# Residual rows and stores of a graph layer: from one DMA queue to halves on two

## The chip, the cores and the metric

The kernel runs on one core of a Trainium2 chip. A core has five engines with a queue of instructions each: TensorE (PE in the profile, its weight loads PEld), VectorE (DVE), ScalarE (ACT), GpSimd (POOL) and SyncE (SP), and 16 DMA engines that all queues share. A DMA is issued by an instruction in the queue of SyncE, ScalarE or GpSimd; an engine's instructions start in their written order, so one that waits holds up all that are queued behind it. The metric is the device time of one execution in microseconds (us).

## The reference

Eight batches of 4096 nodes with 256 features go through one layer of a graph network with a residual connection and a layer norm. With the setup's sizes it is:

```python
HW = jnp.einsum('bnf,fo->bno', H, W)              # H = x: 8 x 4096 x 256, W: 256 x 256
A_norm = jax.nn.relu((A + A.T) * 0.5)             # A = adj: 4096 x 4096, mostly zeros
D = jnp.sum(A_norm, axis=1)
d_inv_sqrt = jnp.where(D > 0, jnp.where(D > 0, D, 1.0) ** (-0.5), 0.0)
DAD = d_inv_sqrt[:, None] * A_norm * d_inv_sqrt[None, :]
L_norm = jnp.eye(N) - DAD
gnn = jax.nn.relu(jnp.einsum('nm,bmo->bno', L_norm, HW))
x = layernorm(x + gnn, axis=-1)                   # no scale or shift, eps 1e-5
```

All numbers are float32.

## The kernel before

**First stage.** The adjacency matrix is symmetrised tile by tile (512 x 512) and written to a scratch array `a_dram` in memory, by DMAs in ScalarE's queue (line 513); the features are multiplied by the weights, scaled and written to `g_dram` (8 KB a node: 8 batches of 256 features), also from ScalarE's queue (lines 622 and 633). The product for the first block of 128 output nodes, `lead`, is summed alongside. Which nodes have any neighbour in which block is noted, and lists of the nodes that matter are made from that.

**Second stage.** The other 31 blocks of 128 output nodes are worked on in 16 units, in the order of `SEQ`: 1 to 7, then 0, then 8 to 15. Unit u holds the blocks 2u+1 and 2u+2 (unit 15 only block 31). For each unit a list of nodes is gathered from memory in tiles of 128: GpSimd issues, per tile, an indirect DMA for pieces of `a_dram` (`ga`, line 944) and one for rows of `g_dram` (`g`, line 952, 1 MB). The tiles lie in a ring of 12 buffers (`RING`), so gathers run ahead of the products.

TensorE's work of a unit is cut into *steps*, written out by `steps_of`. A step is either one full tile (128 rows and columns of the array, four matmuls of 512 columns) or a *tiled* step, in which eight small products, 64 rows by 32 columns, share the array, in four rounds `m`. After each round of a tiled step ScalarE gets an empty instruction, a *tick* (line 1198), that waits for the round's first products; the products of a later round wait for the tick before last. So ticks pass through ScalarE's queue, and TensorE can be at most two rounds ahead of it in tiled steps. Full-tile steps have no ticks.

When a block's last product is done, `finish` is called: ScalarE evicts the four banks to the one buffer `y` with ReLU and the row's scale (`evict`, line 760). One step later follows `rest` on VectorE: it adds `y` to the residual rows (line 770), takes the moments (779, 781), an inverse root by three Newton steps, and normalises in place (line 803, eight instructions, one for each batch). The rows of `x` that are added lie in buffers `xr` of 1 MB, 128 nodes by 8 batches by 256 features; the pool `adj` has four of these. The last block (31) has its own `finish_last`, which evicts (line 1010), adds (1018, 1020, 1026), normalises on ScalarE (1042) and stores in four parts (1049). Its residual rows are loaded by GpSimd's queue into a free ring buffer.

**Order of the work around the change.** Each instruction of the second stage is put, with `queue(...)`, directly behind the one before on its engine. `after(n, fn)` notes a function for later; `run_later(2)` is called once at the end of each step and counts all notes down by two, so `after(2, ...)` means one step on and `after(6, ...)` the third `run_later` from the note. At a new unit the notes are made ahead of that step's own count, so `after(6, ...)` comes at the end of the unit's third step, counted 2 from 0.

Residual rows of blocks 0, 3 and 4 are asked for between the stages, and of block 5 in unit 1's first step. From then on a store brings a load with it: `LATE` = 4, two steps after a block's `rest`, SyncE's queue gets the store of that block (line 813) and behind it the load (line 754) of the block three places further on in `line`, the order in which blocks are finished. A load waits until the buffer's last store has landed. All 31 loads and 31 stores, 1 MB each in pieces of 1 KB, are in SyncE's queue, and ScalarE issues no DMA in this stage.

DMAs of SyncE and ScalarE share eight semaphores in turn: an issue first waits until the DMA that used its semaphore before, eight issues earlier over both queues, has landed.

Of the kernel before, what the change touches and what calls it, by code (L numbers as in the profile page):

```python
# [9 lines left out]
F32 = mybir.dt.float32  # L10
# [13 lines left out]
SEQ = [1, 2, 3, 4, 5, 6, 7, 0, *range(8, 16)]  # L24
# [43 lines left out]
def kernel(  # L68
# [25 lines left out]
    nc = tc.nc  # L94
    B, N, F = x.shape
    FO = w.shape[1]
    P = 128
# [11 lines left out]
    HOLD = 10  # L109
    RING = 12  # L110
    REACH = 5
    LATE = 4
    EPS = 1e-5
    NK = len(KINDS)
    L = 64
# [3 lines left out]
    def blocks(u):  # L119

        return min(2, NB - 1 - 2 * u)
# [104 lines left out]
    for s in range(NE):  # L226
        h = slice((s % QU) * E, (s % QU + 1) * E)
# [240 lines left out]
    blocks_pool = ctx.enter_context(tc.tile_pool(name="adj", bufs=4))  # L468
# [283 lines left out]
    def residual(i, engine):  # L752
        xr = blocks_pool.tile([P, B, F], F32, tag="adj", name=f"xr_{i}")
        engine.dma_start(xr, x[:, i * P : (i + 1) * P, :].rearrange("b p f -> p b f"))
        return xr

    def evict(i, py, ypool):
        y = ypool.tile([P, B, FO], F32, tag="y", name=f"y_{i}", bufs=1)
        for c in range(G // S):
            nc.scalar.activation(  # L760
                y.rearrange("p b o -> p (b o)")[:, c * S : (c + 1) * S],
                py[c],
                AF.Relu,
                scale=minus_r[:, i : i + 1],
            )
        return y

    def moments(i, y, z, stat):

        nc.vector.tensor_add(z, z, y)  # L770
        return statistics(i, z, stat)
# [40 lines left out]
    def store(i, z):  # L812
        nc.sync.dma_start(out[:, i * P : (i + 1) * P, :].rearrange("b p f -> p b f"), z)
# [72 lines left out]
    with (  # L886
# [33 lines left out]
        def queue(engine):  # L920

            traced = reversed(nc.cur_bb.bb.instructions)
            return tc.issue_after(next(i for i in traced if i.engine == engines[engine]))
# [55 lines left out]
        def after(n, fn, *args):  # L979
            later.append((n, fn, args))  # L980

        def run_later(by):
            ready = [l for l in later if l[0] <= by]
            later[:] = [(n - by, fn, args) for n, fn, args in later if n > by]
            for _, fn, args in ready:
                fn(*args)


        line = [0, *(2 * u + 1 + b for u in SEQ for b in range(blocks(u)))]
        u = SEQ[0]  # L990
        xr = {i: residual(i, nc.sync) for i in (0, *range(2 * u + 1, 2 * u + 1 + blocks(u)))}
        for h in range(max(HUBS)):
# [58 lines left out]
        def finish(i):  # L1051

            if i == NB - 1:
                while later:
                    run_later(1)
                finish_last(i)
                return
            with queue("act"):
                y = evict(i, py.pop(i), ypool)

            def rest():
                z = xr.pop(i)
                with queue("dve"):
                    mv, var = moments(i, y, z, stat)
                with queue("dve"):
                    rstd = inverse_root(i, var, stat)

                def end():
                    in_turn(normalise, i, z, mv, rstd)
                    after(LATE, store_late)  # L1070

                def store_late():
                    with queue("sp"):
                        store(i, z)
                    n = line.index(i) + 3
                    if 3 < n < len(line) - 1:
                        residuals([line[n]])

                end()

            after(2, rest)

        def residuals(rows):
            for i in rows:
                with queue("sp"):
                    xr[i] = residual(i, nc.sync)


        ahead = {u: {k: SEQ[n + k] for k in (2, 3, 4) if n + k < NU} for n, u in enumerate(SEQ)}
# [51 lines left out]
        def in_turn(fn, *args):  # L1141

            with queue("dve"):
                fn(*args)

        finish(0)
        ticks = []

# [52 lines left out]
        for q, (u, step) in enumerate(steps):  # L1201
            new = q == 0 or steps[q - 1][0] != u
            if new:
                after(6, prepare, u)
                if q == 0:
                    after(2, residuals, [line[3]])
                left, begun = {}, set()
                for v, st in steps[q:]:
                    if v == u:
                        for _, _, b, j in st:  # L1210
                            for e in range(QU) if j is None else [j]:
                                left[b, e] = left.get((b, e), 0) + 1
                for b in range(blocks(u)):
                    py[2 * u + 1 + b] = []
            touched = sorted({b for _, _, b, _ in step})
            for b in touched:
                if not py[2 * u + 1 + b]:
                    py[2 * u + 1 + b] = [
                        psum.tile([P, S], F32, tag=f"b{b}", name=f"py_{u}_{b}_{c}") for c in range(NC)
                    ]  # L1220
            if step[0][1] is None:
                (op,) = step
                b = op[2]
                hs = {(b, e) for e in range(QU)}
                assert not hs & begun or hs <= begun
                for h in hs:
                    left[h] -= 1
                for c in range(NC):
                    product(
                        u, op, c, slice(0, P), slice(0, P), not hs & begun, not any(left[h] for h in hs)  # L1230
                    )
                begun |= hs
            else:
                for op in step:
                    assert op[2:] in begun
                    left[op[2:]] -= 1
                last = [op for op in step if not left[op[2:]]]
                tiled(u, step, last)
            for op in step:
                t = op[0]  # L1240
                uses_left[u, t] -= 1
                if t < 0:
                    load_hub_rows(SEQ[SEQ.index(u) + 1 :], -1 - t, op[2])
            gather_ahead()
            run_later(2)
            for b in touched:
                if not any(left[b, e] for e in range(QU)):
                    if b == 0:
                        after(2, lists, u)
                    finish(2 * u + 1 + b)  # L1250
        while later:
            run_later(1)


    anyf = ipool.tile([P, 1], F32, tag="anyf", name="anyf")
# [4 lines left out]
    with tc.If(short > 0):  # L1260
        with (
# [4 lines left out]
            for i in range(NB):  # L1266
# [17 lines left out]
                z = residual(i, nc.scalar)  # L1284
                mv, var = moments(i, y, z, stat)
# [30 lines left out]
```

## Time and profile before

| | |
|---|---|
| median of 6 runs | 1511.1 us (1505.04 to 1515.72) |
| the profiled execution | 1512.02 us, span 1509.8 us, mean granted TensorE clock 0.968 |
| second stage, from TensorE's first `py` product | 594.9 us to the end |
| TensorE busy | 1378.6 us, 91% of the span |
| VectorE, ScalarE, GpSimd busy | 69%, 24%, 51% |
| DMA | 543.04 MB, mean 360 GB/s |
| queue of GpSimd (q0), SyncE (q1), ScalarE (q10) | 283.87, 156.25, 100.96 MB |
| evictions of a block, line 760 | 688 ns each, four to a block |
| addition of residual rows, line 770 | 2286 ns each |

The page's busy shares are means over two stages with different limits. In lists of groups a row has the line, engine and operation, what is written and read, the count, the busy time and the mean of one, and then the idle time before them with what ended most of it. In a timeline or chain the first number is the start in us after the span's start, the second the duration; square brackets hold the idle time before and what ended it. The starts of the units, from TensorE's records, are (us): unit 1 594.9, 2 678.3, 3 743.2, 4 804.2, 5 861.6, 6 915.4, 7 973.2, 0 1025.3, 8 1128.3, 9 1179.1, 10 1227.8, 11 1274.4, 12 1324.8, 13 1375.5, 14 1415.0, 15 1453.4.

### The profile page before, as it was taken

How to read it: one execution, taken by the hardware profiler on the slowest of the kernel's cores; microseconds unless marked ns; L12 is line 12 of the kernel's file. 1: busy time of each engine (PE TensorE's matmuls, PEld its weight loads, DVE VectorE, ACT ScalarE, POOL GpSimd, SP SyncE). 2: the span in 40 equal slices, each digit the busy share in tenths (PEclk: the TensorE clock that was granted, in tenths of full speed). 3: DMA queues.
4: the chain of work that ended last, by engine and by line, in shares of the span. 5: the costliest groups of instructions: out<-in, count | busy, mean ns of one | idle time of the engine just before them, and what ended most of it. 6: DMA issues, size and time to landing. Idle time of an engine off the chain costs nothing.

```text
span 1509.8 us, 29675 instructions
## 1 busy us (share of the span) xinstructions
PE 1378.6 (91%) x11008; PEld 746.2 (49%) x11008; DVE 1039.1 (69%) x3173; ACT 360.2 (24%) x462; POOL 769.8 (51%) x1564
## 2 busy tenths in 40 slices
PE   6999998989999979999999999999999998998962
PEld 5877877767777753343433433333333333333320
DVE  5676578979956462319486797798319898989426
ACT  3555544444445441000101101100001011011102
POOL 3444010011313325765765777767656677777741
PEclk9999999999999989999999999999999999999986
DMA  9999999999989999999999999999979999999993
GB/s 360 372 359 400 396 377 349 369 340 350 357 318 349 335 394 382 395 393 317 374 377 337 385 384 369 391 369 384 396 259 329 351 373 401 379 359 391 391 344 133
DMA packets 217158, 543.04 MB, mean 360 GB/s; under 512 B 19369, under 2 KB 109193, under 8 KB 182425
## 3 DMA queue, kind: packets, MB, share of 16 engines
q0 software_dynamic: 55664, 283.87, 49.2%
q1 hardware_dynamic: 122592, 156.25, 30.6%
q10 hardware_dynamic: 38752, 100.96, 17.1%
q8 instruction: 89, 1.46, 0.4%
q14 instruction: 61, 0.50, 0.1%
HBM read 438.03 MB, written 136.34 MB: 380 GB/s over the span
## 4 chain that ended last, share of the span: by engine, by line
PE 45%; DMA 26%; DVE 19%; issue 5%; POOL 2%; ACT 2%; ACTq 0%; SPq 0%; POOLq 0%; DVEq 0%
PE py L1163 28%; PE pg L607 8%; DMA g<-g_dram,gi 7%; DMA xr<-in_x_dram 4%; DMA a_dram<-sym 4%; DVE sym L500 4%; DMA out_dram<-xr 3%; DMA ga<-a_dram,ai 3%; PE lead L565 3%; PE tr L496 3%; DVE sums L507 2%; PE xtr L596 2%; DMA xin<-in_x_dram 2%; DVE stats L779 2%; DVE xr L770 1%
## 5 line engine op out<-in xcount | busy, mean ns | idle before, releaser
L1163 PE MATMUL py<-g,ga 64*32 64x512 f32 (+1 forms) x7136 | 614.2, 609 | 33.8 <-DMA g<-g_dram,gi 16.2
L1163 PEld LDWEIGHTS py<-g,ga 64*32 64x32 f32 (+1 forms) x7136 | 223.6, 113 | 407.5 <-issue 318.4
L952 POOL DMA_INDIRECT g<-g_dram,gi x268 | 298.6, 1114 | 115.6 <-issue 61.6
L944 POOL DMA_INDIRECT ga<-a_dram,ai x268 | 290.6, 1084 | 127.6 <-PE py L1163 61.9
L760 ACT ACTIVATE y<-py,minus_r 128x512 f32<-128x512 f32 x120 | 72.7, 688 | 807.8 <-PE py L1163 524.8
L607 PE MATMUL pg<-w_sb,xt 128*128 128x256 f32 x1024 | 229.4, 382 | 5.8 <-ACT xt L597 4.0
L1163 PE MATMUL py<-g_hub,gh 128*128 128x512 f32 x480 | 220.7, 601 | 5.2 <-DVE pos_k L240 5.2
L500 DVE TENSOR_TENSOR sym<-tr,adj 128x512 f32<-128x512 f32 x256 | 161.5, 680 | 82.0 <-PE tr L496 73.2
L607 PEld LDWEIGHTS pg<-w_sb,xt 128*128 128x128 f32 x1024 | 193.8, 192 | 33.6 <-ACT xt L597 4.4
L508 POOL TENSOR_SCALAR uses<-sums 128x64 uint8<-128x64 f32 x64 | 27.7, 432 | 312.0 <-DVE sums L507 263.6
L507 DVE TENSOR_REDUCE sums<-sym 128x64 f32<-128x2048 f32 x64 | 145.3, 2277 | 51.7 <-ACT sym L504 51.7
L496 PE MATMUL tr<-ident,adj 128*128 128x128 f32 x1024 | 139.7, 286 | 29.1 <-DVE sym L500 17.4
L1163 PEld LDWEIGHTS py<-g_hub,gh 128*128 128x128 f32 x480 | 87.6, 190 | 133.4 <-issue 120.7
L504 ACT ACTIVATE sym<-sym 128x2048 f32<-128x2048 f32 x64 | 122.8, 1918 | 127.7 <-DVE sym L500 127.7
L496 PEld LDWEIGHTS tr<-ident,adj 128*128 128x128 f32 x1024 | 119.7, 147 | 56.0 <-DVE sym L500 35.0
L443 DVE TENSOR_SCALAR low<-lists 128x17 f32<-128x17 f32 (+8 forms) x14 | 2.5, 175 | 197.3 <-PE lists L431 197.3
L770 DVE TENSOR_TENSOR xr<-xr,y 128x2048 f32<-128x2048 f32 x31 | 70.9, 2286 | 70.3 <-DMA xr<-in_x_dram 37.0
L596 PE MATMUL xtr<-ident,xin 128*128 128x128 f32 x512 | 72.4, 287 | 14.9 <-DVE sym L500 14.2
L565 PE MATMUL lead<-gt,strip 128*128 128x512 f32 x176 | 83.0, 594 | 3.3 <-ACT gt L617 3.3
L803 DVE TENSOR_SCALAR xr<-xr,mv,root 128x256 f32<-128x256 f32 x248 | 85.1, 413 | 1.1
L779 DVE BATCH_NORM_STATS2 stats<-xr 128x6 f32<-128x256 f32 x248 | 84.0, 412 | 1.1
L617 ACT ACTIVATE gt<-pg,r 128x512 f32<-128x512 f32 x88 | 60.1, 690 | 77.8 <-PE pg L607 68.1
(157 smaller groups left out, 1060.0 us busy)
## 6 DMA issues: line engine op xcount, KB each, us to landing
adj<-in_adj_dram SPq DMA_DIRECT2D x64, 1024.0 KB
a_dram<-sym ACTq DMA_DIRECT2D x64, 1024.0 KB
xr<-in_x_dram SPq DMA_DIRECT2D x31, 1024.0 KB
out_dram<-xr SPq DMA_DIRECT2D x31, 1024.0 KB
xin<-in_x_dram SPq DMA_DIRECT2D x44, 512.0 KB
g_dram<-gt ACTq DMA_DIRECT2D x22, 1024.0 KB
xin<-in_x_dram POOLq DMA_DIRECT2D x20, 512.0 KB
g_dram<-held ACTq DMA_DIRECT2D x10, 1024.0 KB
```

The lines of the kernel that those rows point to most:

```text
L496: ins = nc.tensor.transpose(pt[:, c * P : (c + 1) * P], tji[:, c, a * P : (a + 1) * P], ident)
L500: nc.vector.tensor_add(sym[:, a, :], pt, tij[:, a, :])
L504: nc.scalar.activation(sym, sym, AF.Relu, scale=0.5)
L507: nc.vector.tensor_reduce(sums, sym.rearrange("p a (c q) -> p a c q", q=E), AX.X, ALU.add)
L565: nc.tensor.matmul(lead[c], lhsT=strip, rhs=g[:, c * S : (c + 1) * S], start=not done, stop=len(done) == NB - 1, skip_group_check=True,)
L596: nc.tensor.transpose(pt[:, k, c, :], xin[b // H][:, b % H + k, c * P : (c + 1) * P], ident)
L607: ins = nc.tensor.matmul(pg[:, k * FO : (k + 1) * FO], lhsT=xt[:, b + k, c, :], rhs=w_sb[:, c, :], start=(c == 0), stop=(c == FC - 1),)
L770: nc.vector.tensor_add(z, z, y)
L779: nc.vector.bn_stats(stats[:, b, :], z[:, b, :])
L944: nc.gpsimd.indirect_dma_start(out=at if both else at[:, : E if one else P], out_offset=None, in_=a_pairs if both else a_groups if one els ...
L952: nc.gpsimd.indirect_dma_start(out=gt, out_offset=None, in_=g_dram, in_offset=bass.IndirectOffsetOnAxis(ap=gi[:, t : t + 1], axis=0), boun ...
L1163: return nc.tensor.matmul(py[2 * u + 1 + b][c][cols, :], lhsT=at[ps, off + cols.start : off + cols.stop], rhs=gt[ps, c * S : (c + 1) * S], ...
```

## The change

Every store of a block and every load of residual rows, but for the three loads between the stages and block 31, is cut into batches 0 to 3 and 4 to 7. One half is issued by SyncE, the other by ScalarE. They are issued in `exchange`: it takes the oldest block that is normalised and not stored (`finished`), stores it, batches 0 to 3 from SyncE, 4 to 7 from ScalarE, and then loads the rows of one block that it is told of, batches 0 to 3 from ScalarE, 4 to 7 from SyncE.

The times of issue change with it. In a unit of two blocks one exchange comes at the end of the third step and one at the end of the sixth, the first with the rows of the unit's own first block, the second with those of its second. Unit 1 has one exchange, at the end of its fourth step, with a store and no load; unit 15 has two without loads, at the ends of its first and second steps. Loads no longer hang on a store three blocks earlier, and block 5's early load in unit 1 is gone. What is left is stored at the end.

```diff
--- before.py
+++ after.py
@@ -109,7 +109,6 @@
     HOLD = 10
     RING = 12
     REACH = 5
-    LATE = 4
     EPS = 1e-5
     NK = len(KINDS)
     L = 64
@@ -986,7 +985,6 @@
                 fn(*args)
 
 
-        line = [0, *(2 * u + 1 + b for u in SEQ for b in range(blocks(u)))]
         u = SEQ[0]
         xr = {i: residual(i, nc.sync) for i in (0, *range(2 * u + 1, 2 * u + 1 + blocks(u)))}
         for h in range(max(HUBS)):
@@ -1053,6 +1051,8 @@
             if i == NB - 1:
                 while later:
                     run_later(1)
+                while finished:
+                    exchange([])
                 finish_last(i)
                 return
             with queue("act"):
@@ -1065,25 +1065,30 @@
                 with queue("dve"):
                     rstd = inverse_root(i, var, stat)
 
-                def end():
-                    in_turn(normalise, i, z, mv, rstd)
-                    after(LATE, store_late)
-
-                def store_late():
-                    with queue("sp"):
-                        store(i, z)
-                    n = line.index(i) + 3
-                    if 3 < n < len(line) - 1:
-                        residuals([line[n]])
-
-                end()
+                in_turn(normalise, i, z, mv, rstd)
+                finished.append((i, z))
 
             after(2, rest)
 
-        def residuals(rows):
+        def exchange(rows):
+
+            if finished:
+                i, z = finished.pop(0)
+                for h, (name, engine) in enumerate((("sp", nc.sync), ("act", nc.scalar))):
+                    bs = slice(h * B // 2, (h + 1) * B // 2)
+                    with queue(name):
+                        engine.dma_start(
+                            out[bs, i * P : (i + 1) * P, :].rearrange("b p f -> p b f"), z[:, bs]
+                        )
             for i in rows:
-                with queue("sp"):
-                    xr[i] = residual(i, nc.sync)
+                t = blocks_pool.tile([P, B, F], F32, tag="adj", name=f"xr_{i}")
+                for h, (name, engine) in enumerate((("act", nc.scalar), ("sp", nc.sync))):
+                    bs = slice(h * B // 2, (h + 1) * B // 2)
+                    with queue(name):
+                        engine.dma_start(
+                            t[:, bs], x[bs, i * P : (i + 1) * P, :].rearrange("b p f -> p b f")
+                        )
+                xr[i] = t
 
 
         ahead = {u: {k: SEQ[n + k] for k in (2, 3, 4) if n + k < NU} for n, u in enumerate(SEQ)}
@@ -1143,6 +1148,7 @@
             with queue("dve"):
                 fn(*args)
 
+        finished = []
         finish(0)
         ticks = []
 
@@ -1202,8 +1208,15 @@
             new = q == 0 or steps[q - 1][0] != u
             if new:
                 after(6, prepare, u)
+                rows = [2 * u + 1 + b for b in range(2)] if q > 0 and blocks(u) == 2 else []
                 if q == 0:
-                    after(2, residuals, [line[3]])
+                    after(8, exchange, [])
+                elif rows:
+                    after(6, exchange, rows[:1])
+                    after(12, exchange, rows[1:])
+                else:
+                    after(2, exchange, [])
+                    after(4, exchange, [])
                 left, begun = {}, set()
                 for v, st in steps[q:]:
                     if v == u:
@@ -1250,6 +1263,8 @@
                     finish(2 * u + 1 + b)
         while later:
             run_later(1)
+        while finished:
+            exchange([])
 
 
     anyf = ipool.tile([P, 1], F32, tag="anyf", name="anyf")
```

## The prediction

> **What bounds the kernel now.** I read the page first (busy shares, chain), then the chain in order of time, the table of waits, the timeline of the last 70 us and SyncE's own timeline; then I counted the matmul records of line 1163 off against the written order of steps, which gives the time of each step.
>
> ```profile
> span 1509.8 us, 29675 instructions
> PE 1378.6 (91%) x11008; PEld 746.2 (49%) x11008; DVE 1039.1 (69%) x3173; ACT 360.2 (24%) x462; POOL 769.8 (51%) x1564
> DMA  9999999999989999999999999999979999999993
> PE 45%; DMA 26%; DVE 19%; issue 5%; POOL 2%; ACT 2%; ACTq 0%; SPq 0%; POOLq 0%; DVEq 0%
> ```
>
> The second stage runs from 594.9 to the end. TensorE is its main bound: a step takes 3.5 to 3.6 us and the units 2 to 5 last little more than their steps. TensorE's pauses over 0.8 us between matmuls sum to about 56 us: 17.5 on gathers (3 us a unit in units 6, 7, 9, 10, 11), 16 on VectorE, and 15.3 in one piece. That piece is in unit 15. The table of waits (us in total, times, longest) and the chain show it:
>
> ```profile
> PE py L1163 <- ACTq L1198: 15.2, 1, 15.2
> ACT y L760 <- DVE xr L770: 167.7, 15, 32.7
> DVE xr L770 <- DMA xr<-in_x_dram: 37.0, 2, 24.3
> ```
>
> ```profile
> 538.19 23.46 DMA xr<-in_x_dram
> ...
> 1382.26 47.06 DMA out_dram<-xr
> 1429.34 42.09 DMA xr<-in_x_dram
> 1471.56 2.30 DVE xr L770
> ...
> 1482.47 2.21 DVE xr L770
> ```
>
> The residual rows arrive late: block 28's let VectorE wait 24.3 us (to 1447.6), block 29's 12.8 us (to 1471.6). There is one y buffer, so ScalarE can't evict block 30 until VectorE has read block 29's y; behind that eviction on ScalarE stand the ticks for which TensorE waits. The timeline of the end:
>
> ```profile
> 1447.64 2.29 DVE L770 TENSOR_TENSOR xr<-xr,y 128x2048 f32<-128x2048 f32 x1 [24.25 <-DMA xr<-in_x_dram]
> 1473.94 2.42 ACT L760 ACTIVATE y<-py,minus_r 128x512 f32<-128x512 f32 x4 [21.49 <-DVE xr L770]
> 1474.12 10.08 PE L1163 MATMUL py<-g,ga 64*32 64x512 f32 x128 [15.21 <-ACTq L1198]
> 1484.79 2.42 ACT L1010 ACTIVATE y<-py,minus_r 128x512 f32<-128x512 f32 x4 [8.42 <-DVE xr L770]
> 1493.20 0.68 DVE L1020 TENSOR_TENSOR g<-g,y 128x512 f32<-128x512 f32 x1
> ```
>
> The loads are late because SyncE's one queue is behind. Its timeline shows issues that should take 0.4 us held for 14 to 16:
>
> ```profile
> 1408.47 17.14 SPq L813 DMA_DIRECT2D out_dram<-xr  x1
> 1429.34 14.34 SPq L754 DMA_DIRECT2D xr<-in_x_dram  x1
> 1444.59 16.29 SPq L813 DMA_DIRECT2D out_dram<-xr  x1
> ```
>
> The packets say why. In 6 us between 1370 and 1388 GpSimd's gathers move some 285 packets (mostly 8 KB, 0.335 us each) and SyncE's queue 340 (1 KB, 0.049 us): about one turn each, so 1 MB of rows takes some 17 us. When the gathers stop at 1468 it takes 4.
>
> **The last units, with the change.** Every engine's program order is written out, so I can place the new instructions. Each exchange puts half a store and half a load on each queue. In the windows of the first stage where SyncE's and ScalarE's queues both work (545 to 550: 661 and 649 packets) they too get about equal turns. With two turns to the gathers' one, a round of 0.385 us for 1 KB becomes 0.435 for 2 KB: 1 MB in some 9.6 us where it took 17.
>
> Unit 14 starts at 1415.0. Its first exchange stands behind step 2 (+10.8 us), its second behind step 5 (+21.3). Blocks 27 and 29 move in the first: 2 MB, about 19 us and 2 to land: block 29's rows are there at 1448. VectorE wants them when block 29 is evicted, 31.6 + 2.6 us into the unit: 1449. Block 30's rows follow in the second exchange, about 1456 if a round is cheaper than I think, 1467 if the gathers last. VectorE is free for them 11.2 us after 1449, at 1460.4. So block 30's addition starts between 1460.4 and 1467; I take 1464, between the two because the gathers end near it. Before, the end hung on 1482.4.
>
> But the change also puts both stores into ScalarE's queue inside unit 15: block 29's after step 0, block 30's after step 1. They wait for VectorE's normalising, and the ticks of the next step are queued behind; TensorE gets two of a step's four rounds ahead and then stops. So from block 30's addition: 10.9 us to its normalising's end (1482.4 to 1493.3 here), 0.6 for the issue, 1.9 for the rest of step 2, 3.5 for step 3, 1.3 for two evictions, and the 16.6 us that now lie between line 1020's start at 1493.2 and the end: 34.8, and 1 for GpSimd's addition: 35.8. The ends are 1496.2, 1499.8 (for 1464) and 1502.8, against 1509.8: **-10 us, -13.6 to -7.**
>
> **The start of the stage.** The fourth early load goes (block 5's, issued at 546.3 and landed by 566). The chain runs through the third, 538.19 for 23.46 us: a DMA waits for the one that last used its semaphore, eight DMAs back over both queues, and ScalarE's store of a_dram issued at 561.7 waits so for the load of block 4. One DMA fewer shifts this by one: that store would wait for block 3's load, landed near 548, and ScalarE would be free at 554.6. But the next store then gets block 4's semaphore, and in ScalarE's queue its wait stands ahead of the second of four gt multiplications (562.74), so most of the stop stays: **-1.3 us**; bounds 0 and -7.5, the whole of the idle time there.
>
> **New waits on ScalarE in the other units.** An exchange costs ScalarE two issues, 0.4 to 0.5 us each by SyncE's unhindered ones, beside an engine that is 24% busy. What counts is the wait: the half store needs the normalising to be done. That ends 11 to 12 us into the next unit for block one (15 in units 4, 11, 12) and 22 to 23 for block two (26 there); the steps before the exchanges end at 10.8 and 21.4 (13 and 23.3). So ScalarE stands 1 to 3 us, and behind it are ticks alone. Full-tile steps need none, and a tiled step runs 1.7 us before it does. What is left over is 0.6 + 0.8 us in unit 8, 0.8 in 10, 2.0 in 11, 1.9 in 12: 6.1 at most. Units 8 and 12 later wait 5 us for VectorE's lists, 10 and 11 some 3 us for gathers, which covers most; without that cover it is all 6.1. **+2, 0 to +6.** SyncE's half waits too, but nothing that it holds up is wanted soon.
>
> Issues that are held cost nothing on SyncE and would stop TensorE on ScalarE. On SyncE they come when over two 1 MB transfers are outstanding; at the start of the run the fourth and fifth of 512-row transfers are held too, 1.5 and 2.5 us, so the limit is about 2000 descriptors. A queue gets four halves in a unit, 2048, of which the first two have some 10 us to drain: nothing held, by this.
>
> **Loads and gathers.** A block's rows are now asked for in its own unit, one block later than before. The first pair should land 20 us after its issue, some 31 us into the unit; VectorE's addition is 46 to 65 us in: covered by 15 us. Until block 30 is loaded the loads are 1 MB further behind, at 380 GB/s 2.6 us of gathers; rounds with two small packets hold the gathers up a little more, and are over sooner. **+1, 0 to +4.**
>
> Sum: -10 - 1.3 + 2 + 1 = -8.3. The profiled execution took 1512.0 us (span 1509.8 and 2.2 around it), 0.9 over the median of 1511.1, in a spread of 1505.0 to 1515.7. So 1503.7 from the profiled one, 1502.8 from the median: **1503**. The terms' ends together, -21 and +3, give this case 1490 to 1514.
>
> **A rule against it.** The trace has one turn for each queue, 340 packets to 285. The Trainium skill's "DMA: Bandwidth & Descriptors" says in "Issuing engines are not separate DMA queues" that transfers run on the same 16 engines whoever issues them, so that spreading them saves only issue time; by that sentence the tail's gain would go. The same page's "Queues, rings and completion order" lets each engine take the rows in turn by packets, which is what the counts look like. The sum above goes by the counts.
>
> **Rivals.** *Two hardware queues share one turn* (against the gathers no faster than one): then block 29's load, now behind block 27's store, lands where both had landed before, near 1472; block 30's near 1479, its addition starts at 1483, and by the 35.8 us the end is 1518 to 1519: +8, **1520**. It decides from an addition of block 30 later than 1474. For it: no window of the trace shows both hardware queues beside full gathers. Against it: 661 and 649. Chance 0.22.
>
> *The gain is covered*: rows come at 1470 and not 1464 (+6), and the ticks' 6 us show in full (+4): 1513, **1512**. For it: slow DMA engines end up to 18 us behind the first. Chance 0.20.
>
> *The start gives more*: the semaphores fall so that ScalarE doesn't stand at 555, -7.5 in place of -1.3: **1497**. Chance 0.13.
>
> That the split is not all the change does is in the sums: stores are later and loads too.
>
> **Chances.** The forecast has 0.45. About 0.5%, 7.6 us, is what a measurement here can tell from no change: faster is below 1503.5, slower above 1518.7. The forecast gives 0.35 faster and 0.10 same; the shared turn 0.22 slower; the cover 0.17 same and 0.03 slower; the start 0.13 faster: 0.48, 0.27, 0.25. The range goes from the forecast's lower part to the shared turn's 1520: 1492 to 1521.
>
> **What would show it.** Right: VectorE's additions of blocks 28 and 29 without idle time on a DMA; TensorE's pause in unit 15 ended by ticks behind a store that waited for line 803, shorter than 15 us; 1 MB of rows in about 10 us beside gathers; no issue on ScalarE over 2 us. Wrong: block 30's addition after 1474, issues held on ScalarE, or pauses on ticks of 2 us and more in most units.

## The result: slightly slower, and where the tail's gain went

The changed kernel takes 1519.2 us (median of 21 runs, 1511.4 to 1523.5) against 1511.5 us before (median of 47): a ratio of 1.0049, 95% interval [1.0036, 1.0062]. The forecast of 1503 pointed the other way. The profiled execution of the changed kernel took 1515.1 us, span 1513.3, which is 3.5 over the span of before; stretches are compared on these two spans, and verdicts come from all runs. That execution is one of the changed kernel's fast ones: of the 7.7 us between the medians the two profiles show 3.5, and where the other 4 lie is not shown.

The lines of the page that answer to those of before:

```profile
span 1513.3 us, 29835 instructions
...
PE 1391.5 (92%) x11008; PEld 744.8 (49%) x11008; DVE 1040.4 (69%) x3173; ACT 360.9 (24%) x462; POOL 772.7 (51%) x1564
...
q1 hardware_dynamic: 92384, 125.32, 24.1%
q10 hardware_dynamic: 69904, 131.89, 22.9%
```

31 MB have gone from SyncE's queue (q1) to ScalarE's (q10). The page's DMA row has the same 40 digits as before: full before, full after. The table of waits (total us, times, longest), first TensorE's waits for gathers before, then after the change:

```profile
PE py L1163 <- DMA g<-g_dram,gi: 16.2, 9, 3.2
```

```profile
ACT y L759 <- DVE xr L769: 112.4, 14, 10.0
...
PE py L1169 <- DMA g<-g_dram,gi: 28.2, 17, 3.4
...
DVE xr L769 <- DMA xr<-in_x_dram: 12.4, 3, 5.8
...
PE py L1169 <- ACTq L1204: 11.5, 9, 3.5
```

Much of what was promised is there. VectorE waits 12.4 us for rows where it waited 37.0, and the one stop of 15.2 us on a tick is gone. In its place stand nine small stops on ticks, and 17 on gathers where there were nine. The timeline of the end shows what was not foreseen:

```profile
1471.36 4.50 PE L1169 MATMUL py<-g,ga 64*32 64x512 f32 x60 [2.34 <-DMA g<-g_dram,gi]
...
1475.04 2.29 DVE L769 TENSOR_TENSOR xr<-xr,y 128x2048 f32<-128x2048 f32 x1 [3.78 <-DMA xr<-in_x_dram]
...
1485.31 9.24 PE L1169 MATMUL py<-g,ga 64*32 64x512 f32 x90 [1.91 <-DMA g<-g_dram,gi]
...
1494.74 2.42 ACT L1008 ACTIVATE y<-py,minus_r 128x512 f32<-128x512 f32 x4 [29.41 <-PE py L1169]
```

Block 30's addition starts at 1475.0, 7.4 us earlier than before, but the last eviction no longer waits for VectorE: its bracket names TensorE. TensorE is late because in unit 15 it now waits for gathers, four times and about 2 us each, and before it did not. It begins a unit earlier. Unit 14's tiled steps 5 to 8 on TensorE, first before, then after:

```profile
1432.58 13.96 PE L1163 MATMUL py<-g,ga 64*32 64x512 f32 x256
```

```profile
1436.90 1.06 PE L1169 MATMUL py<-g,ga 64*32 64x512 f32 x6
1438.59 5.68 PE L1169 MATMUL py<-g,ga 64*32 64x512 f32 x90 [0.64 <-DMA g<-g_dram,gi]
1446.00 2.77 PE L1169 MATMUL py<-g,ga 64*32 64x512 f32 x36 [1.73 <-ACTq L1204]
1450.45 7.09 PE L1169 MATMUL py<-g,ga 64*32 64x512 f32 x124 [1.68 <-DMA g<-g_dram,gi]
```

Four tiled steps run through in 14.0 us before; after, they are broken up and take 20.6, from 1436.9 to 1457.5. Gathers end two of the pauses, a tick the third.

The same count of matmul records as in the prediction cuts each span into stretches: unit 1's start, units 1 to 13, 14, 15, and from the last product to the end of the span.

| us | start of unit 1 | units 1-13 | unit 14 | unit 15 | after the last product | span |
|---|---|---|---|---|---|---|
| before | 594.9 | 820.0 | 38.5 | 30.8 | 25.6 | 1509.8 |
| changed | 590.9 | 828.4 | 45.2 | 30.1 | 18.8 | 1513.3 |
| change | -4.0 | +8.4 | +6.7 | -0.7 | -6.8 | +3.5 |

So two questions are left for the experiments: why the last gathers are late (+6.7 in unit 14; nothing gained in unit 15 although its 15 us stop is gone), and what costs 8.4 us in units 1 to 13.

**The transfers at the end.** GpSimd's gathers can be counted like the steps. The DMA view of the stretch between the issue of gathers 240 (in unit 13) and 264 (in unit 15), first before (1374.7 to 1448.6), then after (1379.8 to 1465.0); the columns of a queue are packets, MB and its share of the 16 engines' time:

```profile
DMA packets 8670, 28.32 MB, mean 383 GB/s; under 512 B 1190, under 2 KB 5603, under 8 KB 5939
...
q0 software_dynamic: 4398, 23.91, 82.8%
q1 hardware_dynamic: 4264, 4.30, 17.0%
```

```profile
DMA packets 12764, 32.87 MB, mean 386 GB/s; under 512 B 1397, under 2 KB 9618, under 8 KB 9954
...
q0 software_dynamic: 4512, 24.55, 73.4%
q10 hardware_dynamic: 4209, 4.18, 14.0%
q1 hardware_dynamic: 4033, 4.01, 13.9%
```

The rate is the same, 383 and 386 GB/s. The gathers' bytes are nearly the same, and 3.9 MB more of rows pass beside them. At 386 GB/s that is 10.1 us, and the stretch is 11.3 longer (85.1 against 73.8). It also begins 5.1 us later, and the last gathered packets land at 1484.7 us instead of 1466.7. Before, one queue had one turn beside the gathers and left those rows for later: counted by packets, 7.4 MB of rows came after gather 264; after the change 3.6 MB do. The late loads among them cost the kernel before its stop of 15.2 us; without that stop units 14 and 15 would have taken it 54.0 us, and the changed kernel, which has none, takes 75.3.

### The profile page after: what moved, and what is told of

It reads as the page before. It is cut to its first block, busy times and chain, and to the rows that moved or that the text cites. A ratio compares the mean times of both kernels' runs of the same rounds, so it can differ in the third digit from the quotient of the medians.

```text
span 1513.3 us, 29835 instructions
## 1 busy us (share of the span) xinstructions
PE 1391.5 (92%) x11008; PEld 744.8 (49%) x11008; DVE 1040.4 (69%) x3173; ACT 360.9 (24%) x462; POOL 772.7 (51%) x1564
## 5 line engine op out<-in xcount | busy, mean ns | idle before, releaser
L1169 PE MATMUL py<-g,ga 64*32 64x512 f32 (+1 forms) x7136 | 627.4, 611 | 41.1 <-DMA g<-g_dram,gi 28.2
L596 ACT COPY xt<-xtr 128x512 f32<-128x512 f32 x128 | 67.8, 593 | 45.2 <-PE xtr L595 43.8
## 6 DMA issues: line engine op xcount, KB each, us to landing
adj<-in_adj_dram SPq DMA_DIRECT2D x64, 1024.0 KB, 11.5
```

Source lines behind the costliest of these rows:

```text
L1169: return nc.tensor.matmul(py[2 * u + 1 + b][c][cols, :], lhsT=at[ps, off + cols.start : off + cols.stop], rhs=gt[ps, c * S : (c + 1) * S], ...
```

## Experiments

Three theories are in the expectations, under varying names. *Ticks*: ScalarE's new waits at the exchanges hold up the ticks (later *waits*). *Times*: the new places of the exchanges matter, not the queues. *Turns*, later *limit*: two queues take more of a full set of DMA engines from the gathers. A pause or stop on a tick, a gather or a list is idle time of TensorE that this ended. All ratios below are to the kernel before on the same chip, with 95% intervals.

**Which queue carries what, first comparison.** The edits set the engine of each half; `one queue` as an example:

```diff
-                for h, (name, engine) in enumerate((("sp", nc.sync), ("act", nc.scalar))):
+                for h, (name, engine) in enumerate((("sp", nc.sync), ("sp", nc.sync))):
...
-                for h, (name, engine) in enumerate((("act", nc.scalar), ("sp", nc.sync))):
+                for h, (name, engine) in enumerate((("sp", nc.sync), ("sp", nc.sync))):
```

One queue, both halves of everything on SyncE:

> The changed kernel with all halves on SyncE: its new times of issue, one queue, no waits on ScalarE. Theory 'turns' (two queues give the row packets two turns to the gathers' one; at a limit of some 366 GB/s the gathers lose what the rows gain): TensorE's pauses on gathers fall from 31.7 us to about 18 as before, the gather numbered 258 (unit 15's first) is issued near 1431 and not 1444, but the last rows come late again: 1510 to 1516 us. Theory 'ticks' (ScalarE's waits for normalising stop TensorE): the 12.6 us of pauses on ticks go, those on gathers stay near 30: 1506 to 1511. Theory 'times' (asking for rows in their own unit in bursts costs the gathers, the second queue does not): as the changed kernel, 1517 to 1521, with pauses on gathers near 30.

The stores' halves on SyncE, the loads' on both:

> The changed kernel with both halves of each store on SyncE, the halves of the loads as they are on both: ScalarE no longer waits for normalising. 'Ticks': nearly all of the 12.6 us of pauses on ticks go and with them the loss, 1506 to 1512. 'Turns': the loads still take two turns and stores one; pauses on gathers 24 to 30, ticks near 0: 1511 to 1517. 'Times': 1517 to 1521 less what ticks were worth.

Everything on ScalarE:

> The changed kernel with all halves on ScalarE: one queue, with all the waits for normalising on ScalarE and twice its issues. 'Turns': pauses on gathers fall to about 18, pauses on ticks rise over 12.6 and issues are held when over some 2000 descriptors stand: 1515 to 1530. 'Ticks': pauses on gathers stay near 30, ticks the same or more: 1519 to 1535. The two are told apart by the pauses on gathers and the issue of gather 258, near 1431 against near 1444 once the ticks' delay is taken off.

Whole stores on SyncE, whole loads on ScalarE:

> The changed kernel with stores whole on SyncE and loads whole on ScalarE: two queues, no waits for normalising on ScalarE; the loads no longer stand behind the stores. 'Turns': two turns only while both a store and a load are under way; rows come at about 17 us for 1 MB, gathers lose about as much as in the changed kernel: pauses on gathers 24 to 32, 1510 to 1517. 'Ticks': 1506 to 1511.

Measured: 0.9984 [0.9959, 1.0008], 0.9976 [0.9948, 1.0004], 1.0357 [1.0322, 1.0391] and 0.9969 [0.9947, 0.9991]. On that chip the granted clock was 0.907 to 0.921 where it is 0.96 to 0.97 in most other profiles, and the kernel before took 1746 us. Tiled steps of eight products took 4.9 us in the median where they take 3.6 elsewhere, and full-tile steps 3.5 on both. TensorE hardly waited for gathers (0.8 us in all with one queue), and so the effect in question could not show. The first, second and fourth kernel differ by less than their intervals. Everything on ScalarE is slower, with 223.8 us of stops on ticks against 163.7 with everything on SyncE: on that chip even a kernel without an issue on ScalarE has many.

**The same again at a clock of 0.97.** The changed kernel itself, and three of the edits:

> The changed kernel itself, as the yardstick for the others of this call, which share its chip and its runs of the kernel before: 1.004 to 1.006 of the time of before, TensorE's pauses on gathers near 30 us and on ticks near 13.

> The changed kernel with all halves on SyncE, where gathers bound the stage (which they did not on the first chip). 'Turns' (two queues give the row packets two turns to the gathers' one): pauses on gathers fall from some 31 us to about 18 and unit 15's first gather is issued at most 3 us later than in the kernel before, the last rows come late: 0.999 to 1.003 of before. 'Ticks' (ScalarE's waits for normalising stop TensorE): ticks' pauses go, gathers stay near 30: 0.996 to 1.000. 'Times' (the new times of issue cost it): 1.004 to 1.006 with pauses on gathers near 30.

> Stores' halves both on SyncE, loads' halves on both, where gathers bound the stage. 'Ticks': 0.996 to 1.000, pauses on gathers unchanged. 'Turns': 1.000 to 1.004, pauses on gathers 24 to 30, on ticks under 2. 'Times': 1.002 to 1.006.

> Stores whole on SyncE, loads whole on ScalarE, where gathers bound the stage: no waits for normalising on ScalarE, two queues at work while a store and a load are both under way. 'Ticks': 0.996 to 1.000. 'Turns': 1.000 to 1.004, pauses on gathers 24 to 32. 'Times': 1.002 to 1.006.

Measured: changed 1.0037 [1.0017, 1.0058]; one queue 1.0076 [1.0052, 1.0099]; stores on SyncE and loads on both 1.0017 [1.0001, 1.0034]; whole loads on ScalarE 0.9969 [0.9954, 0.9984]. With one queue at the new times the rows are late. Its waits:

```profile
DVE xr L769 <- DMA xr<-in_x_dram: 73.1, 7, 21.7
...
PE py L1169 <- DMA g<-g_dram,gi: 9.7, 7, 2.4
```

TensorE waits for gathers 9.7 us in place of 28.2, but that alone does not show whose bytes they had: behind the late rows VectorE makes its lists late, TensorE stands 49.5 us for VectorE, and the gathers gain time. The time is above all three theories. So the new times alone are a loss, and the second queue earns some of it back.

With the stores on SyncE and the loads on both, VectorE waits 62.2 us for rows, TensorE 15.4 us for gathers and, in unit 15, 8.8 us in one piece for a tick; the time is where *turns* had it, but no theory had these waits.

Whole loads on ScalarE are faster than both kernels, by as much as on the first chip. The time is where *ticks* had it, the waits for gathers where *turns* had them:

```profile
PE py L1169 <- DMA g<-g_dram,gi: 25.5, 13, 3.2
...
PE py L1169 <- ACTq L1204: 1.1, 2, 1.0
```

**Exchanges one step later; late stores put off; the split at the old times.** The first takes ScalarE's wait away, since the normalising is done when ScalarE comes to issue:

```diff
-                    after(6, exchange, rows[:1])
-                    after(12, exchange, rows[1:])
+                    after(8, exchange, rows[:1])
+                    after(14, exchange, rows[1:])
```

(and `after(10, ...)` for `after(8, ...)` in unit 1.)

> The changed kernel with every exchange of units 1 to 14 one step later (3.5 us), still on both queues: ScalarE reaches the stores when the normalising is done, at most 3 us of waits are left over before unit 15. 'Ticks' (what the change loses is ScalarE standing at the exchanges): pauses on ticks fall from 13 us to under 4, 0.995 to 0.999 of before, as with the loads alone on ScalarE (0.997). 'Turns' (the second queue takes the gathers' turns): as the changed kernel or 1 to 2 us worse since rows come later, 1.003 to 1.006, pauses on gathers near 27.

The second and third leave the stores of blocks 27 and 28 to unit 15, in the kernel with whole loads on ScalarE and in the changed one:

```diff
-            if finished:
+            if finished and not (rows and rows[0] in (29, 30)):
```

> Loads whole on ScalarE, stores whole on SyncE (0.997 in the last call), and the two stores of unit 14's exchanges left to the two of unit 15 and to the end, so that 2 MB less go beside the last gathers. 'Turns': the last gathers are issued 4 to 6 us earlier, pauses on gathers in units 14 and 15 fall from 11 to some 5 us, and the end comes 3 to 6 us earlier: 0.993 to 0.996 of before. If the last gathers do not hang on the stores: 0.996 to 0.999.

> The changed kernel with the two stores of unit 14's exchanges left to unit 15 and the end, the rest as it is. 'Turns': gathers of unit 15 some 5 us earlier, pauses on gathers in units 14 and 15 down from 12 us to some 6, 0.999 to 1.002 of before. 'Ticks': the same as the changed kernel less the wait in unit 14, 1.002 to 1.005.

The fourth is the kernel before, each store and load issued where it was, but in halves on both queues:

> The kernel before with its stores and loads cut into halves on both queues, at its own times of issue: the split alone. There the store stands two steps behind the normalising's start in ScalarE's queue, 8 us before block one's normalising ends and 11 before block two's, and the load waits for a store that was issued some 11 us earlier. 'Ticks': ScalarE stands 8 to 20 us at each, TensorE's pauses on ticks rise to 100 us and more, 1.05 to 1.15 of before. 'Turns': the same waits are there but count little beside the gathers: 1.00 to 1.03.

Measured: 1.0030 [1.0016, 1.0044], 0.9972 [0.9958, 0.9985], 1.0048 [1.0029, 1.0066], 1.0570 [1.0537, 1.0602]. The last is the clearest of all: two steps after `rest` the normalising is far from done, ScalarE stands, and the ticks stand behind it:

```profile
PE py L1173 <- ACTq L1208: 109.2, 18, 8.8
```

So the new times are what makes halves on ScalarE bearable at all. With exchanges one step later stops on ticks fall from 11.5 to 1.0 us (waits of `py` on line 1204), units 1 to 13 from 828.4 to 821.8 us, and yet the time stays at 1.0030: unit 14 takes 48.6 us. What TensorE gains earlier it hands over to the gathers, for which it now waits 33.4 us in place of 28.2. *Ticks* alone falls.

Putting off the two late stores moved little: the rows in the stretch between gathers 240 and 264 stayed at 8.1 MB in the one and fell from 8.2 to 7.4 in the other. A later place in the written order puts off nothing on SyncE, which has nothing else in its queue and issues a store once its block is normalised. Both times missed what *turns* said, but with the bytes still there the two tell next to nothing about it.

**Late stores left out, early stores left out.** The store in `exchange` is skipped for four blocks, 25 to 28 (handed over in units 13 and 14) or 5 to 8 (units 3 and 4):

```diff
-                for h, (name, engine) in enumerate((("sp", nc.sync), ("act", nc.scalar))):
+                halves = (("sp", nc.sync), ("act", nc.scalar)) if i not in (25, 26, 27, 28) else ()
+                for h, (name, engine) in enumerate(halves):
```

> The changed kernel without the four stores of blocks 25 to 28, which units 13 and 14 hand over; that output is left unwritten. This takes about 4 MB of rows out of the stretch between the issue of gathers 240 and 264, in which the changed kernel moved 8.2 MB of rows beside the gathers in 85.1 us, the kernel before 4.3 MB in 73.8 us. Theory 'limit' (the transfers together move about 383 GB/s there, so each MB of rows that is moved before the last gathers delays them by 2.6 us): the stretch takes 74 to 76 us again, gather 264 is issued near 1455 instead of 1465, and the time is 0.995 to 0.999 of before. Theory 'waits' (ScalarE's stands at the issues delay the evictions, and the gathers are only late because their buffers come free late): the stretch stays above 82 us and the time at 1.003 to 1.006.

> The changed kernel without the four stores of blocks 5 to 8, which units 3 and 4 hand over; that output is left unwritten. As many stores are gone as in the kernel without the late ones, but where TensorE does not wait for gathers. Theory 'limit': hardly any gain, 1.002 to 1.005 of before, the stretch between gathers 240 and 264 at 84 to 86 us. Theory 'waits': as much gain as from leaving out the late ones. If both kernels gain alike, what counts is the number of transfers and not their place.

Measured: 0.9967 [0.9944, 0.9990] without the late ones, 1.0021 [1.0003, 1.0038] without the early ones. Both times are where *limit* put them. As many bytes and issues are gone in both, and the intervals do not overlap: at the end they count for more. The stretch between gathers 240 and 264 (1383.5 to 1463.3) without the late stores:

```profile
DMA packets 8172, 28.41 MB, mean 356 GB/s; under 512 B 1264, under 2 KB 5011, under 8 KB 5347
...
q10 hardware_dynamic: 2112, 2.10, 7.9%
q1 hardware_dynamic: 1527, 1.51, 5.9%
```

It took 79.8 us, between what the two theories said (74 to 76, over 82), at 356 GB/s, and gather 264 was issued at 1463.3, not near 1455: the DMA engines are no longer full and something else holds the gathers, by my reading TensorE itself, which came into unit 14 8.9 us later than in the kernel before. From unit 14's start to the last product this kernel needs 65.6 us, the one without early stores 76.5, the changed one 75.3; but it came into unit 14 5.3 us later than the one without early stores, which gave the gathers time. From unit 1's start to the last product the two differ by 7.8 us (895.7 and 903.5), and the medians by 8.2. It is not the ticks: TensorE's stops on them are 12.3 us without the late stores and 9.1 without the early ones, its waits for gathers 22.2 and 33.3. So four stores beside the last gathers are shown to cost some 8 us more than four early ones (4 to 12 by the intervals); by place, and not by number. That it is their bytes fits the price; a store left out also frees its buffer sooner for a load, and no run parts the two.

**Halves crosswise.** SyncE issues the store's first half and the load's second, ScalarE the load's first and then the store's second, at the changed times and one step later:

```diff
+            if some:
+                move(0, False)      # store, first half: SyncE
+            if rows:
+                move(0, True)       # load, first half: ScalarE
+                move(1, True)       # load, second half: SyncE
+            if some:
+                move(1, False)      # store, second half: ScalarE
```

> The changed kernel with ScalarE's order turned: SyncE issues the store's first half and then the load's second, ScalarE the load's first half and then the store's second, so that a store's half and a load's half are under way together, as where whole stores are on SyncE and whole loads on ScalarE (0.9969 of before). Theory 'mix' (a store beside a load lets the gathers' packets pass faster, 0.327 us instead of 0.334 us for 8 KB): packets of 0.328 us or less, 0.998 to 1.001. Theory 'order' (the halves gain nothing from it, the whole transfers are faster because ScalarE never waits for the normalising and issues half as many): 1.003 to 1.005, packets as in the changed kernel.

> The crosswise halves with every exchange one step later, so that the normalising is done when ScalarE comes to issue. Theory 'mix': 0.995 to 0.998 of before, as good as whole stores on SyncE and whole loads on ScalarE. Theory 'order': 1.003, as the changed kernel with its exchanges one step later (1.0030), with under 2 us of pauses on ticks.

Measured: 0.9987 [0.9967, 1.0008] and 1.0008 [0.9990, 1.0025]. The first is where *mix* put it, and it gives back the loss of the change; but the gathers' 8 KB packets (1180 to 1370 us) took 0.330 us on average, not 0.328 or less, against 0.334 in the changed kernel and 0.327 with whole loads on ScalarE. The second fell between the theories, and is not better than the first although its stops on ticks are fewer (0.8 us against 4.2). Order matters, then; that it works through the packets' duration is not shown.

**The late stores really put off.** After the crosswise runs I tried to give back the bytes. The stores of blocks 27 to 29 are issued, whole, by ScalarE, whose place is tied to the steps by the ticks, after the last step but one of unit 15; once with whole loads on ScalarE, once in the changed kernel:

```diff
-            if finished:
+            if finished and not (rows and rows[0] in (29, 30)):
...
+                last = i in (27, 28, 29)      # both halves on ScalarE if so
...
-                    after(2, exchange, [])
-                    after(4, exchange, [])
+                    after(6, exchange, [])
+                    after(6, exchange, [])
+                    after(6, exchange, [])
```

> Whole stores on SyncE, whole loads on ScalarE (0.9969 of before), but the stores of blocks 27, 28 and 29 are issued by ScalarE after the last step but one of unit 15, when the last gathers have landed (near 1481), and not by SyncE as soon as the blocks are normalised. Theory 'limit': about 2 MB of rows leave the stretch between gathers 240 and 264 (8.1 to 6 MB), which shortens by 5 us; the three stores land between 1481 and 1490, before the last outputs are ready, and cost nothing: 0.992 to 0.995 of before. Theory 'waits' (it is the issues, not the bytes): 0.996 to 0.998, as without the deferral. Slower than that if the late stores hold up the last ones.

> The changed kernel with the same late issue of the stores of blocks 27, 28 and 29, whole, by ScalarE; everything else, halves on both queues included, stays. Theory 'limit': 8.2 to about 6 MB of rows in the stretch between gathers 240 and 264, 5 us less than the changed kernel (1.0037 in the one comparison, 1.0049 in the other): 0.998 to 1.002 of before. Theory 'waits': 1.003 to 1.006.

Measured: 0.9961 [0.9943, 0.9980] and 1.0048 [1.0025, 1.0071]. Both missed what *limit* said and are where *waits* put them. The bytes did leave the stretch (6.2 and 6.3 MB of rows), and TensorE's waits for gathers in unit 15 fell, against the same kernels without the deferral, from 6.4 to 3.8 and from 8.9 to 2.7 us. But the timeline of the first (its profiled execution, 1511.9 us, is its slowest of twelve) shows what took their place:

```profile
1481.45 6.20 ACTq L1081 DMA_DIRECT2D out_dram<-xr  x6
...
1487.76 3.64 PE L1170 MATMUL py<-g,ga 64*32 64x512 f32 x16 [4.78 <-ACTq L1205]
```

Six issues of about 1 us each stand on ScalarE ahead of a tick, and the last step waits 4.8 us for it; in the second kernel's profile as well. I had priced them at nothing. With that stop taken off (an estimate: 4.8 us are 0.0032 of the time), both would be about where *limit* had them; no run was made without it, so whether the deferral pays stays open.

## Why the prediction was wrong, step by step

The second stage's parts, predicted and in the two profiles:

| us | predicted | in the profiles |
|---|---|---|
| start of the stage | -1.3 | -4.0 at unit 1, -0.9 at unit 2 |
| units 2 to 13 (new waits) | +2 | +5.2 |
| loads and gathers | +1 | in the last line |
| units 14, 15 and the tail | -10 | -0.8, loads and gathers included |
| sum | -8.3 | +3.5 |

**The step that failed is "Loads and gathers: +1".** It knew the price, 2.6 us of gathers for each MB at 380 GB/s, and it had the right mechanism for the tail: a second queue gets a second turn. But it counted only the 1 MB by which the loads trail. The stores trail too, and rows that the single queue had left over for the time after the gathers now pass beside them: 3.9 MB in the last stretch, 10.1 us at that price. The sentence on the packets had it in view ("When the gathers stop at 1468 it takes 4", that is 4 us for 1 MB): the kernel before moved much of its rows there, where 1 MB takes 4 us and not 17. What the rows win in turns, the gathers lose, at a sum of 383 to 386 GB/s.

**The tail's term of -10 failed with it.** It let the end hang on block 30's addition, with 35.8 us behind it. That addition starts at 1475.0, 11 us after the 1464 of the sum, outside its bounds (1460.4 to 1467) and 1 us past the point that it named as wrong; by the sum's own 35.8 the end would be 1510.8, and nothing would be gained. Most of the 11 us is a late request. The sum had block 30's rows asked for at 1436.3, 21.3 us into unit 14; ScalarE issued its half of the load at 1445.2, because unit 14 began 4.3 us later and its tiled steps were broken up by the gathers. From there the rows took 29.8 us, where the sum had allowed 27.7. Landings of load halves in the last stretch took some 25 us for an exchange of 2 MB, 12.7 for each MB: faster than the 17 before, slower than the 9.6 of three equal turns.

And the end is 1513.3: a chain that the sum did not hold, the last product at 1494.6 after its waits for gathers, had become the later one. After the last product 6.8 us are saved (25.6 to 18.8), and that is what arrived of the -10; unit 14 took 6.7 of it back. In unit 15 ScalarE did stand at block 30's store, as forecast, until the normalising was done at 1486.0. The line joins the issues of two stores, block 29's and at its end block 30's:

```profile
1471.30 15.06 ACTq L1080 DMA_DIRECT2D out_dram<-xr  x2
```

No stop on a tick came of it, for until 1485.3 TensorE was in the first round of that step, waiting for gathers. So even gathers in time would not have brought the whole -10.

**New waits on ScalarE: right in kind, too small.** Unit 11's second exchange as an example, on ScalarE and VectorE:

```profile
1290.23 2.67 DVE L802 TENSOR_SCALAR xr<-xr,mv,root 128x256 f32<-128x256 f32 x8
...
1292.93 0.38 ACTq L1080 DMA_DIRECT2D out_dram<-xr  x1
...
1293.43 1.51 ACTq L1088 DMA_DIRECT2D xr<-in_x_dram  x1
```

The store half goes out when the normalising ends at 1292.9, as forecast, and its issue takes 0.4 us. The load half's takes 1.5 where 0.4 to 0.5 was taken from SyncE. In the table of waits TensorE's stops on ticks sum to 9.8 us in units 2 to 12, against the 6.1 without cover; the waits for lists in units 8 and 12 did cover part of it (they fell from 10.4 to 3.8 us), and in unit 11 a stop of 3.5 us on a tick took the place of 2.8 us of waits for gathers. Over units 1 to 13 all of TensorE's listed waits rose by 3.4 us only, from 34.2 to 37.6; the other 5 of the 8.4 are in TensorE's busy time, steps that run slower without a pause that the profile shows, and why is open. Six profiles of kernels with the changed exchange need 826.1 to 830.6 us for units 1 to 13, three with whole loads on ScalarE 817.5 to 821.2; a step later it is 821.8, with halves crosswise 819.1, and with both 823.9. So this part, some 8 us, decides which side of the kernel before a version comes out on, and single profiles of equal code differ by 4 us in it. In units 14 and 15 whole loads on ScalarE fare like the changed kernel: 8.1 MB of rows and 85.1 us between gathers 240 and 264. By what rule the order of halves changes the earlier units is open.

**The start.** ScalarE was freed earlier than thought, the stage starts 4.0 us earlier, and 3.1 of it is handed back in unit 1, where TensorE now waits 3.6 us for gathers (0.6 before): the first was issued 2.4 us earlier, the nineteenth 0.2.

**Issues on ScalarE** stayed under 2 us (longest 1.9): right. The second queue takes away SyncE's held issues, 160 us in all before.

**The rivals.** *One shared turn* gave a time of 1520, close to the one measured, for a wrong reason: between 1436 and 1442 us the queues of SyncE and ScalarE moved 411 and 435 packets beside the gathers' 326, far more together than one turn would give. It decided from an addition of block 30 after 1474, and that came at 1475.0, but mostly for a late request, and the end did not hang on it. *The gain is covered* (1512) had the late rows and the uncovered ticks in kind, but not the gathers. *The start gives more* came halfway and was not kept. The case that happened, gathers taking the tail's gain, had its price in the text (2.6 us a MB) and no rival of its own.

**The rule.** The Trainium skill's page "DMA: Bandwidth & Descriptors" says under "Issuing engines are not separate DMA queues" that all transfers run on the same 16 engines and interleave, so that a second issuing engine saves only the issuing. By that sentence the tail's gain would go, and it went; the forecast set the counts of turns against it as if one of the two had to be wrong. The runs show both: the total stayed at 383 to 386 GB/s, and its division among the queues changed with the number of queues, which fits the turns in the same page's "Queues, rings and completion order". In this kernel, whose DMA engines are full, the first sentence gives the sum and the second only says who is late.

## What to carry to other kernels

Where the DMA engines are full, a faster queue is paid for by another one: add up the bytes of all queues in the stretch that matters, divide by the rate that the profile shows there, and ask which transfer is needed last, before counting a gain from turns. A queue that lags may be doing the right thing, if what it carries isn't wanted until the full stretch is over; and a place later in the written order puts nothing off on an engine that has nothing else to do. An issue that waits for data is better on an engine that nobody waits for: whole stores on SyncE and whole loads on ScalarE, the loads needing no normalising, gave 0.9969 [0.9954, 0.9984] of the kernel before, where halves on both gave 1.0037 [1.0017, 1.0058]. It is not all: moving the stores alone to SyncE gave 1.0017, and halves in another order 0.9987.

## What was not expected of the hardware

- The gathers' 8 KB packets took 0.334 us on average in the changed kernel, 0.330 with halves crosswise and 0.327 with whole loads on ScalarE, in the same stretch and at nearly full DMA engines. Other profiles with the changed exchange have 0.336 to 0.337, others with whole loads on ScalarE 0.325 and 0.329, and the kernel before 0.333 with one queue; the median is 0.309 in all but the kernel before (0.312). Why is not shown.
- The granted clock of one of the chips was 0.907 to 0.921 where the others mostly had 0.96 to 0.97; there the kernel before took 1746 us in place of 1511, which is more than the clocks' ratio. One queue at the new times cost nothing there (0.9984, against 1.0076 elsewhere), but whole loads on ScalarE gained the same (0.9969).
- Six store halves issued in a row on ScalarE took 6.2 us, about 1 us each; a single one took 0.4 us.
